# Causal stage of a perceiver layer: mask multiplications shared out, one division for two quads, weight loads in halves

## The chip, the cores and the metric

The kernel runs on one core of a Trainium2 chip. A core has five engines that run side by side, each through its own instructions in a fixed order: TensorE (PE) multiplies matrices, VectorE (DVE), ScalarE (ACT) and GpSimd (POOL) work element by element, and SyncE (SP) issues most of the transfers. An instruction whose operands are not ready holds up everything behind it on the same engine. The matrix products land in PSUM, which this kernel uses as eight banks taken in turn; the other tensors sit in SBUF.

The metric is the time on the device in microseconds, as a median of runs. A profile records one execution: its span runs from the first to the last instruction, and that execution's own time is a little longer than its span.

## The reference

Three residual parts are applied to `x` (4 batches, 256 rows, width 256). The first is cross-attention over a context of 4096 rows with 16 heads. The second, the causal part, is what the change touches: linear attention with positive features, computed within a batch over all earlier rows. The third is a gated feed-forward layer with int32 weights.

```python
x = x + xattn(layernorm(x), ctx, ctx, Wq, bq, Wk, bk, Wv, bv, Wh, bh)     # softmax over 4096
x = x + attn(layernorm(x), Wqkv, bqkv, Wout, bout, omega, nodes, weights)
x = x + ffn(layernorm(x), w_gate, w_up, w_down)

# attn, per head: qf, kf are exp features (64 a head) of the normalised q, k
num = sum over s <= t of (qf[t] . kf[s]) * v[s]
den = max(sum over s <= t of (qf[t] . kf[s]), 1e-6)
out[t] = num / den                          # then @ Wout + bout
# ffn: weights are integers times 1/127
h = silu(x @ wg.T) * (x @ wu.T);  out = h @ wd.T
```

## The kernel before

Everything is float32. The cross-attention fills the first 1081 us of the profiled span. Its last steps already compute, between their own products, most of what the causal part needs for batches 0 to 2: normalised rows, queries, keys, values and the features of the first quads. A quad is four heads of one batch, so there are 4 x 4 = 16 quads, numbered n = 0 to 15, and batch b owns quads 4b to 4b+3.

The stage after that is one loop, written out by hand: in the block at line 509 the instructions of PE, ACT, DVE and SP stand in exactly the order in which the code calls them. GpSimd takes its instructions in the order in which the program emits them. The loop runs over n = 0 to 16. Step n does, in this order: `values` of quad n-1, `scores` of quad n, `divide` of quad n-1, then `features` for two later quads where `early` says so (steps 0, 2, 4, 8, 10), then the pieces that `fills[n]` lists.

`scores` of a quad makes, for each of its four heads, the products of keys and queries in a PSUM tile `pa` of 3 x 128 columns: keys of the first 128 rows against all 256 queries, and keys of the second 128 against the last 128 queries. Only the first and third block need the causal mask; the middle one is kept whole. DVE multiplies each `pa` with a `mask` tile of ones and zeros (line 417) and writes `at` to SBUF. `values` multiplies the four `at` with the values into a PSUM tile `po` (line 426); one row of each head's 32 is the denominator. ACT copies `po` to `avT` (line 431). `divide` transposes `avT` on PE (`pt_o`, line 438), and DVE takes the maximum with 1e-6, the reciprocal and the product (lines 440 to 442) into `att`.

`features` makes four PE products `pf` (line 271), each clipped by DVE (line 277), passed through the exponential on ACT (line 278), with one half scaled on GpSimd (line 279). `output(b)` transposes `att` (`tr_o`), copies it on ACT (`oT`, line 457), multiplies by `wout` (`py`) and adds into `xr`. `feed_forward(b)` normalises (`norm`), transposes (`turn`, `tr_z`, copied by ACT to `zT`), forms `hidden` in three pieces (`pg`, `pu`, lines 488 to 494) and `down` (`pd`, line 500). Batch 3 of the causal part is not prepared early: `project15` finishes the last rows of cross-attention, `norm3` normalises them (a chain of small DVE instructions), `turn3` transposes them (`tr`, copied by DVE to `zT` at line 199) and `qk3`, `v3` project them (`pqk`, `pv`).

The feed-forward weights come in at the beginning of this stage. SP issues the load of one whole matrix of 768 KB into a single buffer `w_i`, and ACT converts and scales it:

```python
def weight(i):
    nc.scalar.activation(ws[i], coming[i], AF.Copy, ...)   # line 390
    if i + 1 < len(ws):
        weight_load(i + 1)
```

The next load is therefore issued when the conversion before it is done. The conversions stand in ACT's order in steps 1, 2 and 3: `weight(0)` first in `fills[1]`, `weight(1)` in `fills[2]` after `turn15`, and `weight(2)` last in `fills[3]`. In step n+1 ACT's next instruction after such a conversion is the `avT` copy of quad n.

Of the kernel before, what the change touches and what calls it, by code (L numbers as in the profile page):

```python
# [12 lines left out]
F32 = mybir.dt.float32  # L13
I32 = mybir.dt.int32
AF = mybir.ActivationFunctionType
ALU = mybir.AluOpType
# [4 lines left out]
P = 128  # L21
B, T, D = 4, 256, 256
S = 4096
H, HD = 16, 16
# [15 lines left out]
def perceiver_layer(  # L40
# [5 lines left out]
    nc = tc.nc  # L46
    const = ctx.enter_context(tc.tile_pool(name="const", bufs=1))

    def load(src, shape, name, dtype=F32, queue=None, pool=const):
        t = pool.tile(shape, dtype, tag=name, name=name)  # L50
        (queue or nc.scalar).dma_start(out=t, in_=src)
        return t
# [13 lines left out]
    ident = const.tile([P, P], F32, tag="ident", name="ident")  # L66
# [4 lines left out]
    for q in range(NQ):  # L71
        for j in range(4):
            h = 4 * (q % 2) + j
            nc.gpsimd.dma_start(
                out=bk_sb[h * HD : (h + 1) * HD, q // 2 : q // 2 + 1],
                in_=bkP[32 * j + 1 : 32 * j + 1 + HD, q : q + 1],
# [98 lines left out]
    def bank(shape, name):  # L175

        return psum.tile(shape, F32, tag="b", name=name)
# [60 lines left out]
    def normed(tiles):  # L238

        some = nrm[:, tiles[0] : tiles[-1] + 1, :].rearrange("p t h -> p (t h)")  # L240
        nc.vector.tensor_scalar(some, some, 1e-24, None, ALU.max)
        y, pieces = inverse_root(some)
        for piece in pieces:
            piece()
        nc.vector.tensor_copy(some, y)

    def qk_normed(t):
        to = qk[t].rearrange("p (h d) -> p h d", d=HD)
        nc.vector.tensor_tensor(to, to, nrm[:, t, :].unsqueeze(2).to_broadcast([P, 2 * H, HD]), ALU.mult)

    def qk_turned(t):
        ps = bank([P, 4, P], "tr_qk")
        for k in range(4):
            nc.tensor.transpose(ps[:, k, :], qk[t][:, k * P : (k + 1) * P], ident)
        nc.vector.tensor_copy(qkT[:, :, t * P : (t + 1) * P], ps)
# [3 lines left out]
    def feature(n, part):  # L259
        i = 2 * (n % 4) + part  # L260
        return kts[2 if n % 8 < 4 else 0][:, i * 2 * T : (i + 1) * 2 * T]
# [103 lines left out]
    late = ctx.enter_context(tc.tile_pool(name="late", bufs=1))  # L365
    work = ctx.enter_context(tc.tile_pool(name="work", bufs=2))

    mask = late.tile([P, 3, P], F32, tag="mask", name="mask")
    nc.gpsimd.memset(mask, 1.0)
    for i in (0, 2):  # L370
        nc.gpsimd.affine_select(
            out=mask[:, i, :], in_=mask[:, i, :], compare_op=ALU.is_ge, fill=0.0, base=0,
            pattern=[[1, P]], channel_multiplier=-1,
        )
    att = late.tile([P, NT, D], F32, tag="att", name="att")
# [4 lines left out]
        late.tile([P, n, m], F32, tag=name, name=name)  # L380
        for n, m, name in ((KC, HID, "wg"), (KC, HID, "wu"), (NH, D, "wd"))
    ]
    coming = []

    def weight_load(i):
        src = (w_gate, w_up, w_down)[i]
        coming.append(load(src, list(ws[i].shape), "w_i", mybir.dt.int32, nc.sync, late))

    def weight(i):
        nc.scalar.activation(ws[i], coming[i], AF.Copy, scale=(1.0, 0.5, 1.0)[i] / 127.0)  # L390
        if i + 1 < len(ws):
            weight_load(i + 1)

    def attend(n):


        b, q = divmod(n, NQ)
        ats, got = [], []

        def scores():  # L400
            for part in range(2):
                f = feature(n, part)
                qf, kf = f[:, :T], f[:, T:]
                pas = [bank([P, 3, P], "pa") for _ in range(2)]
                for j, pa in enumerate(pas):
                    rows = slice(64 * j, 64 * j + 64)
                    nc.tensor.matmul(  # L407
                        pa[:, 0:2, :], lhsT=kf[rows, :P], rhs=qf[rows, :], start=True, stop=True
                    )
                for j, pa in enumerate(pas):  # L410
                    rows = slice(64 * j, 64 * j + 64)
                    nc.tensor.matmul(  # L412
                        pa[:, 2, :], lhsT=kf[rows, P:], rhs=qf[rows, P:], start=True, stop=True
                    )
                for pa in pas:
                    at = work.tile([P, 3, P], F32, tag="at", name="at", bufs=8)
                    nc.vector.tensor_tensor(at, pa, mask, ALU.mult)  # L417
                    ats.append(at)

        def values():  # L420
            po = bank([P, T], "po")
            for i in range(2):
                for j, at in enumerate(ats):
                    c0 = (4 * q + j) * (HD + 1)
                    rhs = at[:, 2, :] if i else at[:, 0:2, :]
                    nc.tensor.matmul(  # L426
                        po[32 * j : 32 * j + 32, i * P : T], lhsT=va[:, 2 * b + i, c0 : c0 + 32], rhs=rhs,
                        start=i == 0, stop=i == 1,
                    )
            oT = work.tile([P, T], F32, tag="avT", name="avT")  # L430
            nc.scalar.copy(oT, po)
            got.append(oT)

        def divide():
            oT = got.pop()
            pt = bank([P, 2, 4, 32], "pt_o")
            for i in range(2):
                nc.tensor.transpose(pt[:, i].rearrange("p j r -> p (j r)"), oT[:, i * P : (i + 1) * P], ident)
            den = work.tile([P, 2, 4], F32, tag="den", name="den")
            nc.vector.tensor_scalar(den, pt[:, :, :, HD], 1e-6, None, ALU.max)  # L440
            nc.vector.reciprocal(den, den)
            nc.vector.tensor_tensor(
                att[:, 2 * b : 2 * b + 2, 64 * q : 64 * q + 64].rearrange("p t (j d) -> p t j d", d=HD),
                pt[:, :, :, :HD], den.unsqueeze(3).to_broadcast([P, 2, 4, HD]), ALU.mult,
            )

        return scores, values, divide

    def output(b):
# [59 lines left out]
    with tc.manual_schedule(engines={ET.PE, ET.Activation, ET.DVE, ET.SP}):  # L509
        normalise, turn15, project15 = finish  # L510
        normalise()
        weight_load(0)
        NB = B * NQ
        fills = {n: [] for n in range(NB + 1)}
        norm3, turn3, qk3, sq3, v3, _ = causal_in(3)
        fills[1] += [lambda: weight(0)]
        fills[2] += [turn15, lambda: weight(1)]
        fills[3] += [project15, norm3, lambda: weight(2)]
        fills[4] += [turn3, lambda: qk3(0)]
        fills[5] += [lambda: qk3(1), lambda: sq3(0), v3, lambda: sq3(1), lambda: normed((6, 7))]  # L520
        fills[6] += [lambda: qk_normed(6), lambda: qk_normed(7)]
        fills[7] += [lambda: qk_turned(6), lambda: qk_turned(7)]
        ff = {}

        def call(b, part, *args):
            return lambda: ff[b][part](*args)

        def begin(b):
            ff[b] = feed_forward(b)
            ff[b][0]()  # L530

        for b in range(B):
            n0 = 4 * b + 4
            turn, down = call(b, 1), [call(b, 3, i) for i in range(2)]
            hidden = [call(b, 2, m) for m in range(NH // 2)]
            fills[n0] += [lambda b=b: output(b), lambda b=b: begin(b)]
            if b < B - 1:
                fills[n0 + 1] += [turn]
                fills[n0 + 2] += [hidden[0]]
            if b < B - 2:  # L540
                fills[n0 + 3] += [hidden[1]]
                fills[n0 + 4] += [hidden[2]]
                fills[n0 + 5] += down
            elif b == B - 2:
                fills[n0 + 3] += [hidden[1]]
                ends = [hidden[2]] + down
            else:
                fills[n0][:0] = ends[:1]
                fills[n0] += ends[1:] + [turn] + hidden + down
        early = {0: 6, 2: 8, 4: 10, 8: 12, 10: 14}  # L550
        steps = [attend(n) for n in range(NB)]
        for n in range(NB + 1):
            if n > 0:
                steps[n - 1][1]()
            if n < NB:
                steps[n][0]()
            if n > 0:
                steps[n - 1][2]()
            if n in early:
                features(early[n])  # L560
            for piece in fills[n]:
                piece()
# [495 lines left out]
```

## Time and profile before

| what | value |
|---|---|
| median of 3 runs | 1235.87 us (1234.32 to 1236.06) |
| the profiled execution's own time | 1238.65 us |
| its span | 1236.9 us, mean granted clock 0.993 |
| PE busy | 1200.7 us (97%) |
| DVE / ACT / POOL busy | 928.3 / 673.2 / 60.2 us |
| PE busy from 1083 to 1120 us (37 us) | 24.1 us |
| PE busy from 1120 to 1205 us (85 us) | 82.7 us |

The page gives the busy time of each engine over the span, and the trace can be asked for the same in any stretch of it, for the instructions of an engine in order of time, and for who waited for whom. "Idle before, and its releaser" of an instruction is the time in which its engine stood still before it and whose end it waited for. The busy share over the whole span is an average over a long first stage and the short one described here, so the stretch has to be looked at by itself.

### The profile page before, as it was taken

To read this page: it belongs to the slowest core of one execution; us is meant where nothing else is said; L and a number is where in the kernel's file an instruction comes from. 1 tells how busy PE (TensorE), PEld (TensorE's weight loads), DVE (VectorE), ACT (ScalarE), POOL (GpSimd) and SP (SyncE) were. 2 spreads that over 40 slices of the span, in tenths; PEclk is the share of its full clock that TensorE was granted. 3 is DMA by queue.
4 is the path that set the end of the run, shared out by engine and by line. 5 is a ranking of instruction groups with operands and counts; after the bars stand their busy time and mean duration, and the time that the engine had idled before them with its cause. 6 is when DMAs were issued, how large, how long until landed. Compare 5 with 4: busy or idle time off the path is not lost.

```text
span 1236.9 us, 42097 instructions
## 1 busy us (share of the span) xinstructions
PE 1200.7 (97%) x17712; PEld 808.3 (65%) x17712; DVE 928.3 (75%) x1823; ACT 673.2 (54%) x1394; POOL 60.2 (5%) x115
## 2 busy tenths in 40 slices
PE   6999999999999999999999999999999999969998
PEld 3557667666776677667766776677667755546777
DVE  5777777777777777777777777777788877487763
ACT  3336666666655665666666665666666646741311
POOL 4010000000000000000000000000000012020100
PEclk9989999999999999999999999999999999999999
DMA  6341332233222322232223222332232000020000
GB/s 229 104 165 69 104 100 84 66 88 108 84 73 85 105 91 73 84 104 94 73 81 105 95 72 80 87 110 74 80 89 97 22 2 4 2 80 1 9 10 18
DMA packets 57756, 95.78 MB, mean 77 GB/s; under 512 B 29024, under 2 KB 31712, under 8 KB 57568
## 3 DMA queue, kind: packets, MB, share of 16 engines
q1 hardware_dynamic: 56384, 92.17, 24.1%
q8 instruction: 140, 2.29, 0.7%
q10 hardware_dynamic: 672, 0.92, 0.2%
q14 instruction: 48, 0.39, 0.1%
q0 software_dynamic: 512, 0.00, 0.0%
HBM read 74.17 MB, written 1.05 MB: 61 GB/s over the span
## 4 chain that ended last, share of the span: by engine, by line
PE 92%; DVE 4%; DMA 1%; ACT 1%; issue 1%; SPq 0%; ACTq 0%; POOL 0%; DVEq 0%
PE pt L741 22%; PE pm L704 18%; PE pav L761 18%; PE pv L668 11%; PE pk L638 10%; PE pd L500 2%; PE pg L488 1%; PE pu L488 1%; PE pq L844 1%; PE pqk L207 1%; PE po L426 1%; PE pa L407 1%; PE py L819 1%; PE py L462 1%; PE pf L271 0%
## 5 line engine op out<-in xcount | busy, mean ns | idle before, releaser
L711 DVE TENSOR_REDUCE mx<-pm 128x1 f32<-128x512 f32 x1024 | 636.1, 684 | 149.2 <-PE pm L704 149.1
L746 ACT ACTIVATE e<-pt 128x512 f32<-128x512 f32 x1024 | 529.0, 603 | 387.2 <-PE pm L704 362.2
L741 PE MATMUL pt<-qa,kt 32*128 32x256 f32 x4096 | 502.5, 389 | 1.7 <-DVE qa L727 1.0
L704 PE MATMUL pm<-kt,qT 32*128 32x512 f32 x2048 | 501.0, 621 | 2.8 <-ACT ku L646 2.8
L741 PEld LDWEIGHTS pt<-qa,kt 32*128 32x128 f32 x4096 | 317.8, 185 | 119.3 <-ACT v L675 43.2
L761 PE MATMUL pav<-e,v 128*32 128x256 f32 x4096 | 269.8, 380 | 0.0
L704 PEld LDWEIGHTS pm<-kt,qT 32*128 32x128 f32 x2048 | 172.7, 185 | 19.9 <-issue 4.9
L761 PEld LDWEIGHTS pav<-e,v 128*32 128x32 f32 x4096 | 128.7, 110 | 73.9 <-ACT e L746 4.7
L771 DVE TENSOR_TENSOR av<-pav,av 128x256 f32<-128x256 f32 x240 | 101.7, 424 | 66.1 <-PE pav L761 65.8
L668 PE MATMUL pv<-wv_sb,ctx 128*32 128x128 f32 x4096 | 138.4, 277 | 0.0
L638 PE MATMUL pk<-ctx,wk_sb 128*32 128x256 f32 x2048 | 138.1, 391 | 0.0
L668 PEld LDWEIGHTS pv<-wv_sb,ctx 128*32 128x32 f32 x4096 | 104.8, 110 | 44.7 <-DVE mx L711 43.5
L638 PEld LDWEIGHTS pk<-ctx,wk_sb 128*32 128x32 f32 x2048 | 55.2, 111 | 69.0 <-DVE mx L711 41.5
L646 ACT ACTIVATE ku<-pk,bk_sb 128x256 f32<-128x256 f32 x128 | 63.0, 495 | 13.7 <-PE pk L638 5.5
L675 ACT COPY v<-pv 128x256 f32<-128x256 f32 x128 | 51.8, 405 | 8.3 <-PE pv L668 8.3
L798 POOL TENSOR_TENSOR on<-on,bv_sb 128x64 f32<-128x64 f32 x32 | 9.2, 308 | 825.9 <-DVE on L793 825.9
L417 DVE TENSOR_TENSOR at<-pa,mask 128x384 f32<-128x384 f32 x64 | 31.1, 549 | 7.0 <-PE pa L412 7.0
L278 ACT ACTIVATE kt<-kt,shift 128x512 f32<-128x512 f32 x32 | 22.4, 725 | 20.9 <-DVE kt L277 20.9
L277 DVE TENSOR_SCALAR kt<-pf,low,top 128x512 f32<-128x512 f32 x32 | 23.7, 803 | 3.0 <-PE pf L271 3.0
L488 PE MATMUL pg<-zT,wg 128*128 128x256 f32 x96 | 23.0, 382 | 0.7 <-ACT zT L480 0.7
L492 ACT ACTIVATE th<-pg 128x512 f32<-128x512 f32 x12 | 7.1, 594 | 29.9 <-PE pg L488 29.9
L488 PE MATMUL pu<-zT,wu 128*128 128x256 f32 x96 | 22.7, 379 | 0.0
(126 smaller groups left out, 563.6 us busy)
## 6 DMA issues: line engine op xcount, KB each, us to landing
ctx<-in_ctxT_dram SPq DMA_DIRECT2D x128, 512.0 KB
kt<-ku SPq DMA_DIRECT2D x500, 32.0 KB
xo<-on SPq DMA_DIRECT2D x128, 8.0 KB
xr<-in_x_dram SPq DMA_DIRECT2D x4, 256.0 KB
out_dram<-o SPq DMA_DIRECT2D x8, 128.0 KB
wqkv_sb<-in_wqkv_dram SPq DMA_DIRECT2D x1, 768.0 KB
w_i<-in_w_gate_dram SPq DMA_DIRECT2D x1, 768.0 KB
w_i<-in_w_up_dram SPq DMA_DIRECT2D x1, 768.0 KB
```

The source lines that it names most:

```text
L417: nc.vector.tensor_tensor(at, pa, mask, ALU.mult)
L488: nc.tensor.matmul(ps[:, i, :], lhsT=w[:, k, ns], rhs=zT[:, k, :], start=k == 0, stop=k == KC - 1)
L638: nc.tensor.matmul(pk[32 * j : 32 * j + 32, :], lhsT=wk_sb[:, k, m * P + 32 * j : m * P + 32 * j + 32], rhs=x[:, k, cs], start=k == 0, sto ...
L646: nc.scalar.activation(ku[:, cs], made.pop(), AF.Identity, bias=bk_sb[:, m : m + 1])
L668: nc.tensor.matmul(pv[32 * j : 32 * j + 32, i, :], lhsT=x[:, k, t0 + 32 * j : t0 + 32 * j + 32], rhs=wv_sb[:, k, m * P : (m + 1) * P], sta ...
L675: nc.scalar.copy(to.rearrange("p t (h d) -> p t h d", d=HD + 1)[:, :, :, :HD], made.pop().rearrange("p t (h d) -> p t h d", d=HD),)
L704: nc.tensor.matmul(pm, lhsT=qT[rows, q, t0 : t0 + P], rhs=kt[rows, c * CH : (c + 1) * CH], start=True, stop=True,)
L711: nc.vector.tensor_reduce(mx[:, i, j, c : c + 1], pm, AX.X, ALU.max)
L741: nc.tensor.matmul(pt[:, i, :], lhsT=kt[rows, ks], rhs=qa[rows, :], start=True, stop=True)
L746: nc.scalar.activation(e, pt, AF.Exp, scale=0.25)
L761: nc.tensor.matmul(pav[32 * h : 32 * h + 32, :], lhsT=v[:, t % KT, c0 : c0 + 32], rhs=es[n, h][:, i, :], start=i == 0, stop=i == 1,)
L771: nc.vector.tensor_tensor(avs[u], pav, avs[u], ALU.add)
```

## The change

Three things change, all in the causal stage.

Masks: of the four `pa` tiles of a quad, the first two (`part == 0`) are no longer multiplied with `mask` by DVE. ACT copies the whole tile to `at`, and GpSimd then zeroes the masked half of blocks 0 and 2 in place with `affine_select`. The other two keep the DVE multiplication.

Division: `got` is shared between quads, `divide` runs only in even steps n = 2, 4, ..., 16, and handles quads n-2 and n-1 together: four transposes into one `pt_o` tile, and one maximum, one reciprocal and one product of twice the size. `avT` gets three buffers.

Weights: each matrix is loaded and converted in two halves of 384 KB. There are two `w_i` buffers, the first two loads are issued together, and `weight(n)` for n = 0 to 5 stands first in `fills[n+1]`, so in steps 1 to 6; each conversion issues the load two halves ahead.

```diff
-    coming = []
-    def weight_load(i):
-        src = (w_gate, w_up, w_down)[i]
-        coming.append(load(src, list(ws[i].shape), "w_i", mybir.dt.int32, nc.sync, late))
-    def weight(i):
-        nc.scalar.activation(ws[i], coming[i], AF.Copy, scale=(1.0, 0.5, 1.0)[i] / 127.0)
-        if i + 1 < len(ws):
-            weight_load(i + 1)
+    coming = {}
+    def weight_load(n):
+        i, half = divmod(n, 2)
+        w = ws[i].shape[1] // 2
+        src = (w_gate, w_up, w_down)[i][:, half * w : half * w + w, :]
+        coming[n] = work.tile([P, w, ws[i].shape[2]], I32, tag="w_i", name="w_i")
+        nc.sync.dma_start(out=coming[n], in_=src)
+    def weight(n):
+        i, half = divmod(n, 2)
+        w = ws[i].shape[1] // 2
+        nc.scalar.activation(
+            ws[i][:, half * w : half * w + w, :], coming.pop(n), AF.Copy, scale=(1.0, 0.5, 1.0)[i] / 127.0
+        )
+        if n + 2 < 6:
+            weight_load(n + 2)
+    got = []
...
                 for pa in pas:
                     at = work.tile([P, 3, P], F32, tag="at", name="at", bufs=8)
-                    nc.vector.tensor_tensor(at, pa, mask, ALU.mult)
+                    if part == 0:
+                        nc.scalar.copy(at, pa)
+                        nc.gpsimd.affine_select(
+                            out=at[:, 0:3:2, :], in_=at[:, 0:3:2, :], compare_op=ALU.is_ge, fill=0.0, base=0,
+                            pattern=[[0, 2], [1, P]], channel_multiplier=-1,
+                        )
+                    else:
+                        nc.vector.tensor_tensor(at, pa, mask, ALU.mult)
                     ats.append(at)
...
-            oT = work.tile([P, T], F32, tag="avT", name="avT")
+            oT = work.tile([P, T], F32, tag="avT", name="avT", bufs=3)
...
         def divide():
-            oT = got.pop()
-            pt = bank([P, 2, 4, 32], "pt_o")
-            for i in range(2):
-                nc.tensor.transpose(pt[:, i].rearrange("p j r -> p (j r)"), oT[:, i * P : (i + 1) * P], ident)
-            den = work.tile([P, 2, 4], F32, tag="den", name="den")
+            pt = bank([P, 2, 8, 32], "pt_o")
+            for m, oT in enumerate(got):
+                for i in range(2):
+                    nc.tensor.transpose(
+                        pt[:, i, 4 * m : 4 * m + 4].rearrange("p j r -> p (j r)"), oT[:, i * P : (i + 1) * P], ident
+                    )
+            got.clear()
+            den = work.tile([P, 2, 8], F32, tag="den", name="den")
...
-        weight_load(0)
+        for n in range(2):
+            weight_load(n)
...
-        fills[1] += [lambda: weight(0)]
-        fills[2] += [turn15, lambda: weight(1)]
-        fills[3] += [project15, norm3, lambda: weight(2)]
+        for n in range(6):
+            fills[n + 1] += [lambda n=n: weight(n)]
+        fills[2] += [turn15]
+        fills[3] += [project15, norm3]
...
-            if n > 0:
+            if n > 0 and n % 2 == 0:
                 steps[n - 1][2]()
```

More of the change, by code (lines that the diff above doesn't have):

```diff
@@ L382, in perceiver_layer @@
     ]
-    coming = []
-    def weight_load(i):
-        src = (w_gate, w_up, w_down)[i]
-        coming.append(load(src, list(ws[i].shape), "w_i", mybir.dt.int32, nc.sync, late))
-    def weight(i):
-        nc.scalar.activation(ws[i], coming[i], AF.Copy, scale=(1.0, 0.5, 1.0)[i] / 127.0)
-        if i + 1 < len(ws):
-            weight_load(i + 1)
+    coming = {}
[14 more added lines that the diff above has]
+    got = []
     def attend(n):
         b, q = divmod(n, NQ)
-        ats, got = [], []
+        ats = []
         def scores():
@@ L442, in divide @@
             nc.vector.tensor_tensor(
-                att[:, 2 * b : 2 * b + 2, 64 * q : 64 * q + 64].rearrange("p t (j d) -> p t j d", d=HD),
-                pt[:, :, :, :HD], den.unsqueeze(3).to_broadcast([P, 2, 4, HD]), ALU.mult,
+                att[:, 2 * b : 2 * b + 2, 64 * q - 64 : 64 * q + 64].rearrange("p t (j d) -> p t j d", d=HD),
+                pt[:, :, :, :HD], den.unsqueeze(3).to_broadcast([P, 2, 8, HD]), ALU.mult,
             )
```

## The prediction

> **What bounds the kernel now.** I read the page first: PE is busy 97% of the span, and the chain that ended last is PE for 92%. The change touches only the end, so I asked for busy time by stretches, cut where the causal stage begins (columns: stretch, length, busy time of PE, weight load, DVE, ACT, POOL, granted clock, DMA share, GB/s):
>
> ```profile
> 1083.00:1095.00 12.00, 7.85 (x92) 5.05 (x88) 9.16 (x19) 4.88 (x7) 2.27 (x6) 1.00 0.25 73
> 1095.00:1102.00 7.00, 4.18 (x54) 2.99 (x54) 5.82 (x12) 4.51 (x6) 1.91 (x4) 1.00 0.30 114
> 1102.00:1114.00 12.00, 6.26 (x60) 4.12 (x60) 10.69 (x34) 4.62 (x6) 3.02 (x6) 1.00 0.19 67
> 1114.00:1120.00 6.00, 5.76 (x20) 2.97 (x22) 1.11 (x2) 0.65 (x2) 1.44 (x2) 0.72 0.00 0
> 1120.00:1137.00 17.00, 16.37 (x133) 11.74 (x132) 15.84 (x54) 2.30 (x5) 1.04 (x1) 1.00 0.00 1
> 1137.00:1205.00 68.00, 66.33 (x526) 52.61 (x522) 50.27 (x133) 15.29 (x30) 3.82 (x8) 1.00 0.03 9
> ```
>
> PE is idle 12.7 us of the first three stretches (31 us) and hardly after that. All that can be won is there, plus the clock loss at 1114. The waits of PE in this stage (total, times, longest) say what for:
>
> ```profile
> PE pt_o L438 <- ACT avT L431: 9.5, 5, 2.8
> PE pqk L207 <- DVE zT L199: 3.8, 1, 3.8
> PE py L462 <- ACT oT L457: 1.7, 4, 0.9
> PE po L426 <- DVE at L417: 0.6, 1, 0.6
> ```
>
> Why is `avT` late? ACT in order of time (start, length, line; the bracket is idle time before it and its releaser):
>
> ```profile
> 1092.86 1.48 ACT L390 ACTIVATE wg<-w_i 128x1536 f32<-128x1536 int32 x1 [4.06 <-DMA w_i<-in_w_gate_dram]
> 1094.24 0.35 ACT L431 COPY avT<-po 128x256 f32<-128x256 f32 x1
> ...
> 1099.88 1.47 ACT L390 ACTIVATE wu<-w_i 128x1536 f32<-128x1536 int32 x1
> 1101.25 0.35 ACT L431 COPY avT<-po 128x256 f32<-128x256 f32 x1
> 1105.41 1.48 ACT L390 ACTIVATE wd<-w_i 128x1536 f32<-128x1536 int32 x1 [3.81 <-DMA w_i<-in_w_down_dram]
> 1106.80 0.35 ACT L431 COPY avT<-po 128x256 f32<-128x256 f32 x1
> ```
>
> Each time ACT sits on a weight conversion, twice waiting for its transfer, with `avT` queued behind it and PE's `pt_o` behind that. The prices for the new work come from these groups (busy us, mean ns):
>
> ```profile
> L417 DVE TENSOR_TENSOR at<-pa,mask 128x384 f32<-128x384 f32 x64 | 31.1, 549 | 7.0 <-PE pa L412 7.0
> ...
> L480 ACT COPY zT<-tr_z 128x512 f32<-128x512 f32 x4 | 2.3, 585 | 26.8 <-PE tr_z L479 26.8
> ...
> L371 POOL TENSOR_SCALAR_AFFINE_SELECT mask<-mask 128x128 f32<-128x128 f32 x2 | 0.5, 292 | 0.1
> ```
>
> And the clock, halved after PE's longest gap (1109.88 to 1113.67), until about 1117.4:
>
> ```profile
> 1114.00:1115.00 1.00, 1.00 (x2) 0.34 (x1) 0.00 (x0) 0.00 (x0) 0.40 (x1) 0.50 0.00 0
> ```
>
> [...] one gap of 3.79 us, then 0.50 for about 3.4 us; the gaps of 2.8 us and less did not do it. [...] 366 ns for 256 elements and 585 for 512, so 0.15 us + 0.85 ns. [...] In the early steps DVE reads PSUM or takes 0.16 us instructions, so I give this nothing[...].
>
> **The change part by part, each priced alone.** ACT copy of 384 elements: between 366 and 585 ns, 475. GpSimd select of 2x128: at least the 292 of 1x128, at most twice that; I take 450 (0.9 us a quad). DVE loses two of four mask products a quad, 2 x 0.465 start to start = 0.93 us. Division: per pair three DVE instructions fewer, 0.16 + 0.20 + 0.29 = 0.65 us, against some 0.15 us of longer ones; PE's 32 transposes stay, moved by one step (0.37 us out of each odd step, into each even one, sum zero). Half conversion: 0.82 to 0.84 us (1482 ns less 768 elements at 0.83 to 0.86), two of them 0.2 us dearer than a whole. Half load: the whole ones took 4.34 and 4.04 us from issue to release, with about 2.45 us of transfer visible in the GB/s slices; half of that off gives 3.0 us. SP issues it at 1088.52 as before, behind the same eight row transfers, so the first half is there at 1091.5 and the second near 1092.8.
>
> **The walk.** Added singly these say little, since the engines wait on each other; so I put the new order through the queues with the durations of the trace, from 1081.9 (unchanged up to there). X(n) is the start of `scores` of quad n on PE.
>
> Step 0: DVE begins the clips 0.4 us earlier (1084.45), exponentials end at 1088.15. Step 1: `avT`(0) 1088.45, copies of quad 1 to 1089.3, behind the exponentials; GpSimd has its four scalings until 1088.75, then the two selects to 1089.85. So `values`(1), which waited for DVE before, now waits for GpSimd: X(2) = 1090.65 against 1090.46. No gain yet, rather 0.2 lost.
>
> Step 2: first half converted 1091.5 to 1092.35, `avT`(1) 1092.65 (before: 1094.6). `pt_o` 1092.7 to 1093.45 with four transposes, `pf` to 1094.5. DVE: division to 1094.4, clips to 1097.3, `px` copy to 1097.6. PE meanwhile X(3) = 1095.7 against 1097.25.
>
> Step 3: `py` for the last cross-attention rows 1097.65 to 1098.6, its DVE add to 1099.1 (before: 1103.41, since `py` stood behind the wait of 2.82 us), then `norm3`, 4.15 us as in the trace, to 1103.25. PE waits 1.6 us for the selects of quad 3 (exponentials to 1098.05, second half 0.85, `avT`(2), copies to 1100.0, selects to 1100.6), X(4) = 1101.3 against 1103.67. That wait is hidden under `norm3`: quad 4's products are there at 1102.85.
>
> Step 4: DVE two masks to 1104.25, division to 1105.0, four clips to 1107.9, `zT` to 1108.5. Before: four masks from 1107.64, `zT` done at 1113.61. So PE starts `pqk` 5.1 us earlier, after a gap of 3.2 us in place of 3.79. ACT's oT is behind exponentials to 1108.7 and a half conversion to 1109.5, in time.
>
> After that PE is the bound again. `pqk` to the end of `py` took 6.3 us at the halved clock; at full clock `pqk` is 1.72 instead of 3.3 us, about 1.65 less in all. Steps 5 to 8: in step 6 before, `values` waited 0.63 us for `at` and was then stretched to 2.2 us from 0.8; DVE, with one mask pair less and one division skipped, is there at 1127.1 when PE comes at 1127.5, which removes 2.0 us. Moved transposes leave +0.4 at that point. `values`(7) starts at 1134.2 against 1141.79, 7.6 earlier; ACT's oT in step 8 comes 0.14 earlier. From step 9 on PE has no waits of size to lose. ACT's two copies cost it nothing there: they follow `avT`, and the fill of every step gives PE at least 3.46 us until `values` needs them; without that cover 1.9 us a step would show. In step 16 the transposes of quad 14 fill 0.37 us of the 0.55 us wait for `avT`. Sum: 5.1 + 2.0 + 0.4 + 0.1 + 0.4 = about 8.1 us with the clock halved again at `pqk`, 9.8 us without.
>
> Against the profiled execution (span 1236.9, itself 1238.65) that is a span of 1227.1 to 1228.8. The median of the runs shown is 2.8 us below that execution. If its runs paid the halved clock too, the full 9.8 applies to 1235.87: 1226.1; if they did not, 8.1: 1227.8. I take 1227.0.
>
> **Rivals.** *The halves land together.* If the two transfers of one queue share the engines evenly, the first half is there with the second, at about 1092.85. `avT`(1), `pt_o` and the DVE chain down to `zT` follow 1:1: gain 6.8 to 8.4, near 1228.5. For it: both are issued within 0.4 us.[...]
>
> *GpSimd's select is dear, moderately.* At 1.0 us, `values`(1) and (3) come 1.1 us later each; `pt_o` absorbs half a microsecond of the first and `norm3` 1.5 us of the second with what it hides, so about 1.3 us lost: 1228.3. At 1.5 us about 4 us: 1231.
>
> *Slower: GpSimd becomes the bound.* In a filled step the two copies end 1.9 us after X(n) and PE needs the result at X(n) + 5.0. Above 1.55 us a select, every step with only a `hidden` piece pays twice the excess, and the first five steps pay about 6 to 7 us together. At 1.75 us the sum is about 8 us and the gain is gone; at 2.2 us it ends near 1241. For it: the strided in-place form over two blocks is nowhere in the trace of before. Against: six times the 292 ns measured for half the elements.
>
> *The early chain stays bound elsewhere.* If DVE's chain in steps 2 to 4 does not move up (a wait that I overlook, between `pt_o` and `zT`), only step 6 and the masks remain: gain about 4, 1232.
>
> **How the numbers follow.** Main case 0.60 (1225 to 1228.5, both clock variants), halves together 0.12, select moderately dear 0.10, early chain bound elsewhere 0.08, slower 0.05; and 0.05 for more than 10.5 us won, should the gaps in steps 1 and 3 close too. The range 1223.5 to 1231.0 leaves out the slower case, most of the chain that stays bound and a sliver below. What this measurement can tell from no change is about 0.2%, 2.5 us. Faster by that: all but the slower case and the worst of the dear select and of the bound chain, 0.91; within it 0.04; slower 0.05.
>
> **What would show it.** In the profile after: the first `wg` conversion starts near 1091.5 and lasts 0.8 us; `at` copies on ACT near 0.47 us, selects near 0.45; PE's wait for `avT` falls from 9.5 to below 1.5 us; a new wait of `po` for GpSimd's `at`, 3 to 5 us in steps 1 and 3; `zT` done 5 us earlier and the clock at `pqk` mostly 1.00; DVE's group at the mask halved to 32, 15.5 us. I am wrong if the selects are above 1 us, if the first half lands after 1092.5, or if PE waits anew from step 5 on.

## The result, and the profile after

The changed kernel takes 1230.04 us (median of 9 executions, 1227.98 to 1234.11), the kernel before, run beside it, 1236.20 us (9 executions, 1234.32 to 1238.39). The ratio is 0.9951, 95% interval 0.9937 to 0.9964: about 6 us less. A second comparison, run later, gave 1229.49 us (6 executions) against 1237.82 (11), ratio 0.9935 (0.9919 to 0.9950).

The two profiled executions seem to say more: the span is 1226.3 us after and 1236.9 before, 10.6 less. But 4.3 us of that come before the causal part begins, where nothing was changed: PE's first product `pa` starts at 1077.56 us after and at 1081.90 before, and 3.9 of these are there by 91 us: the clock granted to PE at the beginning differed (between 80 and 90 us it was 0.66 before and 1.00 after). So I compare the stage alone, from PE's first `pa` to the end of the span. It is 155.0 us before and 148.7 after, 6.3 less, which is what the medians say. To put a time of the trace after beside one of before or of the prediction, add 4.34 us.

Busy time by stretches of the profile after (columns: stretch, length, busy time and instructions of PE, weight load, DVE, ACT, POOL, granted clock, DMA share, GB/s):

```profile
1078.66:1104.66 26.00, 17.51 (x203) 11.97 (x199) 20.38 (x49) 15.98 (x30) 10.97 (x25) 1.00 0.28 80
1104.66:1109.66 5.00, 4.76 (x11) 2.30 (x12) 0.69 (x1) 1.40 (x4) 1.07 (x2) 0.66 0.26 79
```

The poorly filled stretch, from 1.1 us after the first `pa` (1083.00 before, 1078.66 after) to the start of `pqk`, is now 26 us long instead of 31, and PE is idle in it for 8.5 us instead of 12.7. The waits of PE in this stage (total, times, longest):

```profile
PE pqk L207 <- DVE zT L199: 4.0, 1, 4.0
PE po L443 <- POOL at L429: 3.6, 2, 2.4
PE py L482 <- ACT oT L477: 1.3, 4, 0.6
...
PE pt_o L455 <- ACT avT L448: 0.2, 1, 0.2
```

The wait for `avT`, 9.5 us before, is gone. A new one for GpSimd has come, 3.6 us in two places, and the wait for `zT` before `pqk` is about as long as it was (3.97 us against 3.79). Why `avT` is on time shows in ACT in order of time:

```profile
1087.31 0.84 ACT L395 ACTIVATE wg<-w_i 128x768 f32<-128x768 int32 x1 [2.33 <-DMA w_i<-in_w_gate_dram]
1088.06 0.35 ACT L448 COPY avT<-po 128x256 f32<-128x256 f32 x1
...
1093.63 0.83 ACT L395 ACTIVATE wg<-w_i 128x768 f32<-128x768 int32 x1
1094.36 0.35 ACT L448 COPY avT<-po 128x256 f32<-128x256 f32 x1
```

The first half starts at 1091.65 on the scale of before (forecast 1091.5). ACT waits there for the transfer, which costs PE the 0.2 us for `avT` above; the later halves wait for no transfer at all. The new and the changed work, in groups from 1081 us to the end (busy us, mean ns; the first two of each 32 lie earlier):

```profile
L434 DVE TENSOR_TENSOR at<-pa,mask 128x384 f32<-128x384 f32 x30 | 15.3, 550 | 13.3 <-PE pa L422 13.2
L428 ACT COPY at<-pa 128x384 f32<-128x384 f32 x30 | 12.9, 482 | 6.0 <-PE pa L422 6.0
L429 POOL TENSOR_SCALAR_AFFINE_SELECT at<-at 128x256 f32<-128x256 f32 x30 | 11.8, 407 | 62.7 <-ACT at L428 62.6
```

A copy costs 482 ns (forecast 475), a select 407 ns (forecast 450).

### The profile page after: what moved, and what is told of

It is laid out like the page before. It is cut to its first block, busy times and chain, and to the rows that moved or that the text cites. A ratio compares the mean times of both kernels' runs of the same rounds, so it can differ in the third digit from the quotient of the medians.

```text
span 1226.3 us, 42061 instructions
## 1 busy us (share of the span) xinstructions
PE 1195.3 (97%) x17712; PEld 806.3 (66%) x17712; DVE 911.9 (74%) x1767; ACT 686.8 (56%) x1429; POOL 72.7 (6%) x147
## 4 chain that ended last, share of the span: by engine, by line
PE 92%; DVE 5%; ACT 1%; DMA 1%; issue 1%; ACTq 0%; DVEq 0%
PE pt L763 22%; PE pm L726 18%; PE pav L783 18%; PE pv L690 11%; PE pk L660 10%; PE pd L520 2%; PE pg L508 2%; PE pu L508 1%; PE pq L866 1%; PE pqk L207 1%; PE pa L417 1%; PE py L841 1%; PE py L482 1%; DVE kt L277 1%; PE po L443 1%
## 5 line engine op out<-in xcount | busy, mean ns | idle before, releaser
L733 DVE TENSOR_REDUCE mx<-pm 128x1 f32<-128x512 f32 x1024 | 635.9, 684 | 145.3 <-PE pm L726 145.2
L434 DVE TENSOR_TENSOR at<-pa,mask 128x384 f32<-128x384 f32 x32 | 16.3, 550 | 14.2 <-PE pa L422 14.1
L520 PE MATMUL pd<-wd,hT 128*128 128x256 f32 x96 | 21.6, 381 | 0.0
```

Of the source, the lines that this page charges most:

```text
L520: nc.tensor.matmul(pd, lhsT=hT[:, n, i * P : (i + 1) * P], rhs=wd[:, n, :], start=n == 0, stop=n == NH - 1)
L733: nc.vector.tensor_reduce(mx[:, i, j, c : c + 1], pm, AX.X, ALU.max)
```

## The experiments

All times of the stage below run from PE's first `pa` to the end of the span; those of single instructions are taken from the first `pa` too where this is said.

### Each part alone, and each part undone

The three parts were put into the kernel before singly:

```diff
 # weights alone: halves of weight(), two w_i, and
-        weight_load(0)
+        for n in range(2):
+            weight_load(n)
...
+            fills[n + 1] += [lambda n=n: weight(n)]
 # masks alone
-                    nc.vector.tensor_tensor(at, pa, mask, ALU.mult)
+                    if part == 0:
+                        nc.scalar.copy(at, pa)
+                        nc.gpsimd.affine_select(out=at[:, 0:3:2, :], in_=at[:, 0:3:2, :], ...)
+                    else:
+                        nc.vector.tensor_tensor(at, pa, mask, ALU.mult)
 # division alone
-            if n > 0:
+            if n > 0 and n % 2 == 0:
                 steps[n - 1][2]()
```

> The kernel before with the weight halves alone (masks all on VectorE, one division per quad). Measure: the stage, from the first score product on PE to the end of the span, 155.0 us before and 148.7 with all three parts. My theory: the parts share the gain, and no part is worth the whole. Walk: first half there at 1091.5 in the time of before, avT(1) done 2.0 us earlier, zT for pqk at 1111.0 against 1113.6; the wait for at in step 6 stays. Stage 152.3 (-2.7). Rival: the conversions are the cause of all waits, so this part alone brings 5 us or more: stage 150 or less. The opposite rival, that VectorE's chain sets the end and the halves bring nothing: 154.5 to 155.5.

> The kernel before with the masks alone (half by ScalarE and GpSimd), whole weights and a division per quad. My theory: the weights still hold avT until 1094.6, 1101.6 and 1107.2, so zT comes only about 1 us earlier; the wait and the stretched values in step 6 go (2 us). Stage 152.0 (-3.0), with PE's wait for avT still above 8 us. Rival (VectorE's load is the cause, so the masks carry the gain): stage 150 or less. Rival (halves carry everything): 154.5 or more.

> The kernel before with the paired division alone. My theory: the even steps' transposes still wait for avT behind the conversions, but PE no longer waits for avT(0) and avT(2), so the projection of the last rows and norm3 start about 1.3 us earlier; zT about 1.0 earlier, and 0.65 of VectorE's work is out of step 5. Stage 153.3 (-1.7). Rival (division is off the path): 154.6 to 155.4.

Then each was taken out of the changed kernel, the other two staying (the diffs are those above, read backwards):

> All but the weight halves: the part undone. My theory: zT about 1.2 us earlier than before, the step 6 wait gone, stage 151.8 (-3.2), so the halves are worth 3 us on top of the others. Rival (weights carry nearly all): stage 154 or more. Rival (weights bring nothing): stage 149.

> The changed kernel with the masks undone: DVE multiplies all four tiles of a quad, ACT's copies and GpSimd's selects are gone; halves of the weights and the double division stay. Theory (moving half of the masks off DVE shortens its chain to zT by one mask pair in steps 2 and 4, and removes DVE's lateness in step 6): zT 28.8 us after the first pa in place of 26.96, the wait of po in step 6 back (0.6 us and the stretch after it), stage 151 us in place of 148.7. Rival (what DVE saves, the waits of po for GpSimd take back): zT 27.0 and stage 148.7 or less.

> The changed kernel with the division undone (`divide` in every step for one quad, two `avT` buffers); halves and masks stay. Each pair of steps gives DVE 0.65 us more. Theory (the division is a small help to DVE, felt only where DVE sets the pace, in step 4 ahead of zT and in step 6): zT about 0.5 us later than the changed kernel's 26.96 after the first pa, step 6 about 0.7 longer, stage 150 us in place of 148.7. Rival (what counts is that PE doesn't stop for pt_o in odd steps: with avT again wanted one step after it is made, behind exponentials and half conversions): waits of PE for avT of 2 us or more in steps 1, 3 and 5, zT 28.5 or later, stage 151.5 or more, as much as undoing either of the other two parts.

What was measured:

| in the kernel | median, before beside it | ratio (95%) | stage | halved stretches in it | `zT` done | wait for `avT` |
|---|---|---|---|---|---|---|
| nothing (before) | | 1 | 155.0 us | 1 | 31.7 us | 9.5 us |
| weights | 1233.31, 1237.49 | 0.9976 (0.9965 to 0.9986) | 154.0 | 3 | 29.9 | 5.1 |
| masks | 1235.25, 1237.49 | 0.9986 (0.9977 to 0.9996) | 155.0 | 3 | 33.4 | 9.8 |
| division | 1236.54, 1237.49 | 0.9993 (0.9981 to 1.0005) | 156.5 | 4 | 34.0 | 7.0 |
| masks, division | 1233.91, 1237.49 | 0.9972 (0.9962 to 0.9982) | 152.0 | 2 | 32.5 | 3.1 |
| weights, division | 1233.66, 1236.21 | 0.9980 (0.9968 to 0.9991) | 151.9 | 2 | 28.4 | 0.7 |
| weights, masks | 1232.64, 1236.65 | 0.9967 (0.9954 to 0.9979) | 151.3 | 2 | 28.5 | 4.8 |
| all three | 1230.04, 1236.20 | 0.9951 (0.9937 to 0.9964) | 148.7 | 1 | 27.0 | 0.2 |

The stage is that of one profiled execution, and "halved stretches" counts the stretches of 3.4 us with the clock at 0.50 in its first 40 us (one of 6.8 us as two); the next experiment shows what they cost, a microsecond or more each, and that they are partly chance. Measured by the stage, as the expectations have it, the single parts miss: weights alone 154.0 us for 152.3, and masks alone (155.0) and division alone (156.5) are no shorter than before, as their rivals had it. But three and four halved stretches lie in these stages against one before, so the stage probably understates the parts, and I changed to the ratio for the gain (of 1236 us): weights alone 3.0 us (1.7 to 4.3), masks alone 1.7 (0.5 to 2.8), division alone 0.9 (-0.6 to 2.3). They sum to 5.6, against 6.1 (4.4 to 7.8) for the whole. Undone from the whole, they are missed by 2.6 us (weights), 3.6 (masks) and 2.0 (division), in all 8.2. Each of these differences carries an error of about 2 us, so whether the parts help each other isn't settled. By the times, weights and masks have a share in the whole; the division's 0.9 and 2.0 are not clear of zero. (With the second comparison of the changed kernel averaged in, 0.9943, the 2.0 becomes 3.0 and is clear of it.) Its share shows in the profiles below. I had expected 2.7, 3.0 and 1.7 of them alone. The weights part is itself a bundle, of half size, a second buffer and new places in ACT's order; these were not taken apart.

`zT`, expected about 1 us earlier with masks alone and division alone and 1.2 with both, came later in all three (33.4, 34.0 and 32.5 us against 31.7). In all three a halved stretch lay on the `pf` of step 2, which took 2.09 us instead of 1.15, and that pushes back what follows; how much of the delay this explains stays open.

What each alone leaves standing shows in the profiles. In the kernel with the division alone, ACT in order of time:

```profile
1103.98 1.48 ACT L390 ACTIVATE wd<-w_i 128x1536 f32<-128x1536 int32 x1 [5.33 <-DMA w_i<-in_w_down_dram]
1105.38 0.35 ACT L433 COPY avT<-po 128x256 f32<-128x256 f32 x1
```

Here the pair's second `avT` stands behind a whole conversion that waits 5.33 us for its transfer. PE's longest wait for `avT` became 4.6 us: with one division for two quads, a late `avT` holds up both. With the masks alone, whole conversions still stand ahead of `avT`, and the wait for it is 9.8 us. With masks undone from the whole, the waits of PE read:

```profile
PE pqk L207 <- DVE zT L199: 4.0, 1, 4.0
...
PE pf L271 <- DVE at L426: 1.4, 1, 1.4
PE po L435 <- DVE at L426: 1.0, 1, 1.0
```

Now DVE is late: it has four masks before the clips, and PE stops in step 4 in the middle of `pf` for it. The 1.0 us of `po` lie in step 1; in step 6, where I had expected the wait of 0.6 us back, `po` is only stretched, to 2.08 us. With the division undone, PE in order of time:

```profile
1084.91 0.44 PE L452 MATMUL pt_o<-ident,avT 128*128 128x128 f32 x2 [1.58 <-ACT avT L445]
...
1095.37 0.44 PE L452 MATMUL pt_o<-ident,avT 128*128 128x128 f32 x2 [2.12 <-ACT avT L445]
```

These are steps 1 and 3, in which the double division leaves no `pt_o`. The stage, 151.3 us, holds one halved stretch more than the changed kernel's and so doesn't decide between 150 and 151.5. `zT` does, since no clock was halved before 27.0 us, when PE was already waiting for it: 28.5 us is the rival's value, 1.6 later than with the double division where the theory had 0.5. The division does save DVE work, but by this profile its larger worth is that PE doesn't stop for `avT` in the odd steps. In the prediction that effect is in the walk, but not in the prices.

### The halved clock at `pqk`

In the profile after, PE's gap before `pqk` is 3.97 us and `pqk` takes 3.68 us. Two runs ask what the clock had to do with that gap. One is the changed kernel once more:

> The changed kernel as it is, to compare with on the same chip: ratio to before 0.995; in its profile the work up to pqk as in the first one, but the halved clock elsewhere or not at all[...]; stage 147 to 150 us.

The other fills the gap:

```diff
             for i in range(2):
                 for k in range(KC):
                     nc.tensor.transpose(ps[:, k, i, :], z[:, i, k * P : (k + 1) * P], ident)
+            if b == 3:
+                idle = bank([P, 2 * D], "idle")
+                for _ in range(4):
+                    nc.tensor.matmul(idle, lhsT=z[:, 0, :P], rhs=rest[3][:, 0, : 2 * D], start=True, stop=True)
             nc.vector.tensor_copy(zT.rearrange("p k (i t) -> p k i t", t=P), ps)
```

> The changed kernel with four throwaway products of 512 columns on PE between the transposes of z and pqk, into a PSUM tile that nothing reads (additional work, result as before): PE's gap of 3.97 us before pqk is cut to about 2 us, and nothing else moves. Theory (the long gap halves the clock at pqk): pqk 2.0 us in place of 3.68, clock 1.00 in every slice from 1105 to 1112, stage 147.0 us in place of 148.7. Rival (the clock falls whatever PE does there, or the gap costs nothing): pqk 3.3 us or more, stage 148.7 or a little longer.

With the gap filled, the median is 1227.84 us (4 executions) against 1236.21, ratio 0.9928 (0.9908 to 0.9947). PE in order of time:

```profile
1086.15 1.88 PE L447 MATMUL po<-at,va 128*32 128x256 f32 x16 [2.44 <-POOL at L433]
...
1102.56 3.60 PE L203 MATMUL idle<-wqkv_sb,z 128*128 128x512 f32 x8
1106.70 1.98 PE L211 MATMUL pqk<-wqkv_sb,zT 128*128 128x512 f32 x4 [0.54 <-DVE zT L199]
```

`pqk` is back at 1.98 us. The theory holds. The stage is 148.1 instead of the expected 147.0 because the clock was halved elsewhere, after the gap of 2.44 us in step 1: `po` there took 1.88 us (1.23 in the first profile after), and `zT` came 1.1 us later. The changed kernel run again shows that this has nothing to do with the filling. It has the same gaps (2.43 and 3.97 us) and a stage of 149.7 us, with the clock halved after both. Since its first halved stretch begins at almost the same place as in the filled run (7.49 and 7.60 us after the first `pa`), the two can be laid side by side: `pqk` 3.62 and 1.98 us, stage 149.7 and 148.1. The changed kernel run again, in stretches of 3.41 us on both sides of the two places where its halved clock begins:

```profile
1083.28:1086.69 3.41, 1.07 (x14) 0.80 (x11) 2.50 (x5) 3.35 (x7) 2.28 (x5) 1.00 0.11 10
1086.69:1090.10 3.41, 3.32 (x26) 2.17 (x28) 0.00 (x0) 0.22 (x1) 0.41 (x2) 0.50 0.68 220
1103.76:1107.17 3.41, 0.00 (x0) 0.00 (x0) 3.41 (x5) 2.68 (x4) 1.38 (x3) 1.00 0.00 0
1107.17:1110.58 3.41, 3.31 (x4) 1.41 (x5) 0.04 (x1) 0.93 (x2) 0.53 (x2) 0.50 0.37 103
```

And the first profile after around the same gap, in stretches of 3.41 us counted back from its own halved one:

```profile
1080.77:1084.18 3.41, 1.92 (x27) 1.41 (x17) 3.36 (x6) 3.10 (x6) 1.56 (x4) 1.00 0.16 18
1084.18:1087.59 3.41, 2.46 (x31) 1.79 (x32) 0.00 (x0) 1.08 (x4) 1.13 (x3) 1.00 0.70 226
```

The same gap of 2.4 us was followed by the halved clock in one execution, where PE was busy for 1.07 of the 3.41 us before, and not in the other, where the gap lies in two of these stretches, busy for 1.92 and 2.46 us, and the clock stayed at 1.00. Which of the two happens differs between executions of the same kernel. It moved the stage by 1.0 us between these two.

### The select and DVE

> The changed kernel without GpSimd's select: in half of the tiles the causal mask is left out, ACT's copy alone makes at. Theory (the select stands on the path only in steps 1 and 3, and there step 3 is hidden under norm3): the two waits of po for GpSimd (1.2 and 2.4 us) shrink by 0.8 us each, X(2) and zT come 0.8 us earlier, later steps lose nothing; stage 147.7 to 148.1 us in place of 148.7. Second theory (the selects also slow DVE[...] in every step): DVE's 0.16 us instructions of norm are 0.16 everywhere, and the stage is 147.0 or less. Rival (the selects are wholly hidden): 148.7 within 0.3.

```diff
                     if part == 0:
                         nc.scalar.copy(at, pa)
-                        nc.gpsimd.affine_select(out=at[:, 0:3:2, :], in_=at[:, 0:3:2, :], ...)
```

The median is 1228.85 us against 1236.21, ratio 0.9938 (0.9919 to 0.9957), which by itself doesn't part it from the changed kernel. The profiles do. By the stage alone, 148.4 us, the rival would hold (148.7 within 0.3), but this run has one halved stretch more than the profile from which that number was taken. Its clock was halved in nearly the same two places as in the changed kernel run again (8.13 and 28.61 us after the first `pa`, against 7.49 and 27.97), so these two can be laid side by side: stage 148.4 against 149.7, `zT` 0.35 us earlier, and from `po` of step 6 to that of step 7 it takes 6.8 us in place of 7.5. Without the selects, DVE in step 6:

```profile
1122.97 0.19 DVE L241 TENSOR_SCALAR nrm<-nrm 128x64 f32<-128x64 f32 x1
1123.19 0.20 DVE L123 TENSOR_SCALAR ir_y<-nrm 128x64 int32<-128x64 int32 x1
1123.42 0.20 DVE L124 TENSOR_SCALAR ir_y<-ir_y 128x64 int32<-128x64 int32 x1
```

and the same in the changed kernel, first profile after, where GpSimd's two selects of that step run from 1119.58 to 1120.36:

```profile
1119.36 0.20 DVE L241 TENSOR_SCALAR nrm<-nrm 128x64 f32<-128x64 f32 x1
1119.59 0.45 DVE L123 TENSOR_SCALAR ir_y<-nrm 128x64 int32<-128x64 int32 x1
1120.07 0.34 DVE L124 TENSOR_SCALAR ir_y<-ir_y 128x64 int32<-128x64 int32 x1
```

Two instructions of 0.20 us take 0.45 and 0.34 under the selects. The same happened in step 5, under the selects from 1113.21 to 1113.99:

```profile
1113.31 0.31 DVE L128 SCALAR_TENSOR_TENSOR ir_t<-ir_t,ln_v 128x2 f32<-128x2 f32 x1
1113.66 0.34 DVE L129 SCALAR_TENSOR_TENSOR ir_y<-ir_t,ir_y 128x2 f32<-128x2 f32 x1
```

Both take 0.16 us without selects. Each of the four ended 0.01 to 0.05 us after the select beside it. DVE has no idle time between these two places and the masks of step 6, so its chain is 0.33 + 0.39 = 0.72 us longer there, and in step 6 it sets the pace: its masks for `po` end at 1123.91, 0.34 us after PE begins `po`, which then takes 1.23 us in place of 0.86, and the `tr_qk` after it waits for DVE too. So both theories have a share: the waits for GpSimd shrink by 0.47 and 0.42 us (to ACT's 1.96 and 0.72), less than the 0.8 I expected, since ACT's copies stay, and 0.7 us comes from DVE being let alone in steps 5 and 6. The rival, wholly hidden, falls, by the comparison of these two profiles.

### A version that is faster than both

DVE's copy of `zT` stands behind four clips that have nothing to do with it:

```profile
1100.97 2.96 DVE L277 TENSOR_SCALAR kt<-pf,low,top 128x512 f32<-128x512 f32 x4
1103.84 0.68 DVE L199 COPY zT<-tr 128x512 f32<-128x512 f32 x1
```

They belong to quad 10, which is wanted six steps later. The first run moved them to step 7, the second spread all features over steps 8, 10 and 12, and the third filled two gaps as well:

```diff
-        early = {0: 6, 2: 8, 4: 10, 8: 12, 10: 14}
+        early = {0: 6, 2: 8, 7: 10, 8: 12, 10: 14}     # first
+        early = {0: 6, 2: 8, 8: 10, 10: 12, 12: 14}    # second and third
...
+        fills[1] += [lambda: idle(2)]                  # third: two products of 512 columns
+        fills[4] += [turn3, lambda: idle(2), lambda: qk3(0)]
```

> The changed kernel with `features` of quad 10 moved from step 4 to step 7 (nothing left out). In the changed kernel DVE has zT's copy (start 1103.84) behind the four clips of these features (1100.97 to 1103.9), and PE stands still 3.97 us before pqk. Theory (after the change the end is still set by DVE's order in step 4, and the clock at pqk by the length of that gap): zT ends 2.9 us earlier after the first pa (24.1 in place of 26.96 us); PE gets pf's 1.1 us back in step 7, so 1.8 us remain; the gap is then about 2.1 us, pqk runs at full clock (2.0 us in place of 3.68), 1.7 us more: from the first pa to the end of the span 145.2 us in place of 148.7. Rival 1 (something else holds zT: norm3 or the transposes): zT within 1 us of before, stage 148 to 149. Rival 2 (the clips in step 7 come too late for quad 10, PE waits anew there): zT earlier as said, but stage 147 or more with a new wait of PE between steps 7 and 10.

> The changed kernel with the features of quads 10, 12 and 14 in steps 8, 10 and 12 instead of 4, 8 and 10 (nothing left out). With them in steps 4 to 7 the run before this one got 2.8 us at zT and lost 1.9 us again in step 7, where the four pf took 2.27 us in place of 1.15, waiting for DVE's clips. Theory (step 7 is a step in which DVE has just enough time, steps 8, 10 and 12 have more): zT 24.1 us after the first pa; pf 1.15 us in each of the three steps, one of them new in step 12; so 2.85 - 1.1 = 1.75 us remain: stage 146.9 us with pqk at the halved clock, 145.3 without. Median 1.7 us below that of the changed kernel. Rival (DVE has no room there either, or the exponentials come too late for quads 10 and 14): PE waits for pf or pa in steps 8 to 14, stage 148 or more.

> As the run with the features in steps 8, 10 and 12, with two throwaway products of 512 columns on PE (0.9 us each) in step 1, where PE waits 2.4 us for GpSimd, and two in step 4 before pqk, where it waits 1.9 us (additional work). Theory (a gap of PE can halve its clock for the 3.4 us after it[...]; filling the gaps takes that chance away): clock 1.00 in every slice from the first pa to the end, pqk 2.0 us, no instruction stretched; stage 145.3 us, and a median 3 to 4 us below that of the changed kernel, of which 1.7 are the features. Rival (the clock's loss has nothing to do with the gaps, or the medians hardly contain it): median as that of the run without throwaway products.

First run: 1229.59 us against 1236.21, ratio 0.9946 (0.9922 to 0.9969), stage 147.6 instead of 145.2. `zT` came at 24.1, as expected. Two things failed, both shown by PE in order of time:

```profile
1103.89 3.51 PE L207 MATMUL pqk<-wqkv_sb,zT 128*128 128x512 f32 x4 [1.91 <-DVE zT L199]
...
1125.38 2.27 PE L271 MATMUL pf<-qT,om_sb 32*128 32x256 f32 x16
```

A gap of 1.91 us was followed by the halved clock (0.50), and in step 7 `pf` takes 2.27 us instead of 1.15, because there DVE comes late to the clips that set its banks free. So the second rival was right about step 7.

Second run: 1227.68 us against 1237.82, ratio 0.9917 (0.9900 to 0.9934), and 1.8 us below the changed kernel beside it (1229.49); 1.7 were expected. `pf` takes 1.15 us in all three new places. The stage of its profile is 147.4 (expected 146.9), with `pqk` at half clock; step 12 got 1.6 us longer, not 1.1.

Third run: 1226.47 us, ratio 0.9918 (0.9899 to 0.9937), with the stage of its profile 145.9 (expected 145.3). PE:

```profile
1082.98 1.98 PE L544 MATMUL idle<-wqkv_sb,ident 128*128 128x512 f32 x4
1085.49 1.23 PE L443 MATMUL po<-at,va 128*32 128x256 f32 x16 [0.52 <-POOL at L429]
...
1102.18 1.98 PE L207 MATMUL pqk<-wqkv_sb,zT 128*128 128x512 f32 x4 [0.20 <-DVE zT L199]
```

From the first `pa` to the last product its profile has no halved stretch. The median is 3.0 us below that of the changed kernel, the lower end of what I expected. Against the second run, however, the intervals overlap almost wholly, so in the medians the gain from filling gaps is not established here; only what it does to the clock in the profile is shown. Two of its six executions took 1230.59 and 1229.85 us, with a mean clock of 0.993 and 0.994 where the others have 0.997 to 0.999, so clock was still lost in some; where isn't known, since only one execution was traced.

## Why the prediction was right, and where it was not

The kernel is faster, as forecast, and the time, 1230.04 us, is inside the range of 1223.5 to 1231.0. But it is 3.0 us above the 1227.0 and outside the main case (1225 to 1228.5): about 6 us came where 8.9 were forecast. The range held because it had room for the rivals. The sum "8.1 us with the clock halved again" is the one to compare, since the clock was halved (its terms add up to 8.0): the stage got 6.3 us shorter.

**The walk through steps 1 to 4** held to 0.4 us everywhere (on the scale of before, forecast in brackets): X(2) 1090.63 (1090.65), `avT`(1) done 1092.75 (1092.65), X(3) 1095.41 (1095.7), `py` 1097.69 (1097.65), X(4) 1101.12 (1101.3), `norm3` 1103.55 (1103.25), `zT` 1108.86 (1108.5). So `zT` came 4.75 us earlier, not 5.1. The new wait for GpSimd was 3.6 us (3 to 5), that for `avT` 0.2 (below 1.5). The prices of copy, select and half conversion were off by 7, 43 and at most 20 ns. Of the 0.3 us that `norm3` came late, 0.18 were there when it began (its first operand, DVE's add, was done at 1099.28, forecast 1099.1), and 0.12 are its two `z` products, which took 0.86 us together under the selects in place of 0.74. The prediction's 0.15 us + 0.85 ns an element, taken from two of ACT's copies, gives 476 ns for the copy of 384 elements, which took 482, but 585 for 512, where the exponentials took 722: it is a price for copies.

**The step that failed: "so I give this nothing"**, said of GpSimd and DVE at the SBUF. I argued from early steps, in which DVE reads PSUM, and only in one direction, GpSimd waiting for DVE. The trace shows the other: in steps 5 and 6 four DVE instructions took 0.31 to 0.45 us beside the selects, and each ended 0.01 to 0.05 us after the select beside it; without the selects they take 0.16 to 0.20. Why they are held that long was not shown. My forecast had DVE ready at 1127.1 in step 6, before PE; its masks ended at 1128.25, late by the 0.35 of `zT`, the 0.72 under the selects and 0.1 more. That step's wait and stretch (2.0 us) were therefore removed by only some 1.2 us: `values`(7) started at 1135.37, not 1134.2, with 0.35 of the difference from `zT` and 0.37 in the stretched `po` of step 6. The run without selects gives 0.7 of it back.

**The clock.** "The clock at `pqk` mostly 1.00" was wrong, in both profiles of the changed kernel. I read a threshold out of one execution ("one gap of 3.79 us ... the gaps of 2.8 us and less did not do it") and expected 3.2 us to pass mostly. The gap was 3.97, since PE was done 0.4 us earlier and `zT` 0.35 later than I had them; and the gap's length alone doesn't decide: 1.91 us was followed by the halved clock twice, and 3.05 us with masks and division was not (`pqk` took 1.98 us). The term that I had priced right is its cost, about 1.7 us at `pqk`, shown by the filled gap.

**The tail.** I had counted 0.5 us for steps 8 and 16. Of it 0.2 came: `values`(7) is 6.42 us earlier and the stage's last `o` 6.64, and from there to the end of the span it took 0.31 us more in this profile. So 8.1 less 0.35 for `zT`, 0.8 for steps 6 and 7, 0.3 in the tail and 0.3 after the last `o` is 6.3.

**The rivals.** Halves landing together fell with the first conversion at 1091.65; a dear select, and GpSimd as the bound, with 407 ns; the chain bound elsewhere with `zT` at 27.0 us after the first `pa` instead of 31.7.

## What to carry to other kernels

Put the new order through the queues instead of adding prices: the walk met every event of steps 1 to 4 within 0.4 us, where the price of the division alone (0.65 us of DVE a pair) would have missed what it does for PE in the odd steps. Before work is moved from DVE to GpSimd, look for the place where DVE sets the pace on short SBUF instructions, for there the moved work can come back in part, as 0.7 us of it did here. And compare profiles by stage, from a common event, with the halved stretches counted, before a difference of spans is believed.

## What the runs showed of the hardware that was not expected

The same kernel doesn't get the same clock in every execution. In these profiles the clock of PE was at 0.50 for 3.4 us at a time (in before from 1113.98, in the first profile after from 1104.68), and also for 6.8 us (weights alone, from 1107.22) and 10.2 us (division alone, from 1104.77).

Neither the length of PE's gap nor its busy time just ahead tells by itself what follows. A gap of 1.91 us before `pqk` was followed by the halved clock in the first two runs with the features moved; the gap of 2.4 us in step 1 was in the changed kernel run again, and was not in the first profile after; the gap of 3.05 us before `pqk` with masks and division was not. In the 3.41 us ahead of the halved clock PE was busy for 0.10 us in the first profile after, for 0.31 in before and for 1.72 with the features of quad 10 in step 7; after stretches of the same length with 1.51 us (before, 1103.74 to 1107.15) and 1.49 us (masks and division, 1109.91 to 1113.32) the clock stayed at 1.00. And in before, ahead of this stage, it was halved at 83.16 us after 3.41 us in which PE was busy for 2.40.

What sets these cases apart these figures don't show. An idle stretch of about 2 us can cost the 1.6 us by which `pqk` was longer at half clock (3.62 us against 1.98), or nothing, and a profile taken once shows one throw of it.
